# A cleared tile behind each gather, and less room for descriptors, in a graph-attention kernel

## The chip, the cores and the metric

The kernel runs on one core of one Trainium2 chip. Its engines are named as in the profile: PE (TensorE, with PEld for its weight loads), DVE (VectorE), ACT (ScalarE), POOL (GpSimd) and SP (SyncE). The metric is the device time of one launch in microseconds. The time before is 1312.44 us, the median of three runs.

## The reference

The kernel computes one layer of attention on a graph, a residual, and a second normalisation. There are N = 3125 nodes of 128 features, E = 100000 edges sorted by their destination, five relations and eight heads of 16 features. Cut to what matters:

```
for r in range(R):                        # five relations
    mask = edge_types == r
    q = x[dst] @ W_Q[r];  k = x[src] @ W_K[r];  v = x[src] @ W_V[r]   # per head
    logits = (q * k).sum(-1) / 4 + attn_bias[r]
    attn = softmax of logits over the edges of one destination with mask
    out += segment_sum(attn * v, dst)
h = out @ out_proj_w.T + out_proj_b + x
y = layernorm(h) * ln_gamma + ln_beta
return layernorm(x + y)
```

## The kernel before

**Rows instead of edges.** Keys and values are worked out once per node and relation and stored in device memory as `kv_d` (line 532 on), queries likewise as `q_d` (L714), the queries in three bf16 parts. For each tile of 128 edges, POOL fetches the 128 rows of keys and values with one indirect DMA (L865); the row numbers are in `idx`. The queries come as 120 consecutive rows (`qw`, L764, on SP's queue), which PE spreads over the edges with a matrix of zeros and ones (`hot`, L751; matmul L938).

**Steps.** The edges are cut into groups of 512 (four tiles). `NST` = 66 steps handle three groups each, the first only one. `tiles[k]` lists the tiles that step k gathers: 4, 12, 12 and then mostly 11, because in 63 steps one tile (the "early" tile) is not gathered but computed from rows of x that were fetched in the preparation: `early_turn` (L1052), `early_turned` (L1056), `early_rows` (PE, L1063) and `early_keep` (ACT, L1070). That makes 719 gathers in all. The rows of a step lie in one of four slots, two in `kv_early` and two in `kv_late` (made at L829, in memory that the preparation gave back).

**One step.** `products` (DVE, L951 and L958) multiplies keys with queries; `logits` (L999) sums over each head's features; PE turns the logits (L1031), DVE scans them for the maximum per destination (`scans`, L1076 and L1079), `less_max` (L1088), exponentials on ACT, turned back by PE (L1103); `weigh` (L1119) multiplies the values; `places` (ACT, L1132 and L1136) makes the matrix that `sums` (PE, L1146 and L1151) uses to add the edges of a node; `norm` (DVE, L1168 to L1172) divides; `relations` (PE, L1188) and `by_node` (ACT, L1192) put the result in order of nodes. Projection and the normalisations follow in blocks of 128 nodes.

**Order of the work.** The order is written out by hand in one loop over the steps; each engine runs its instructions in that order, and semaphores hold an instruction back until what it needs is there. The gathers are handed out at `POINTS` = 11 points a step. `point(k, j, leave)` issues as many gathers as are due with a lead of `KV_LEAD` = 2.0 steps, and `leave` is an instruction of the step behind which the gather is put. Points 6 to 10 of step k - 1 stand in step k before points 0 to 5 of k. For every step:

```
        point(k - 1, 6, products(k))
        point(k - 1, 7, weighted)
        ...
        point(k - 1, 8, logits(k))
```

**Startup.** The preparation (pools `load`, `work`, `pps` and others, closed together by `pre.close()`, L825) makes the tables. Its last instructions on DVE work out where the rows of each tile begin (L437 to L447) and count violations of the layout (L634 to L665); L671 to L673 add these up. The pool `flow` is opened behind `pre.close()`, so its tiles lie in memory that the preparation used. The gathers of steps 0 and 1 (16 of them) stand behind that in the text, but go to `kv_early`, which is memory of its own.

Of the kernel before, what the change touches and what calls it, by code (L numbers as in the profile page):

```python
# [9 lines left out]
F32 = mybir.dt.float32  # L10
# [8 lines left out]
P = 128  # L19
# [61 lines left out]
def gnn_kernel(  # L81
# [19 lines left out]
    with tc.manual_schedule():  # L101
        windowed_path(
            tc, n_bad_i, x, src, dst, edge_type, w_q, w_k, w_v, attn_bias, out_w, out_b,
            gamma, beta, out,
        )
# [37 lines left out]
def windowed_path(  # L143
# [4 lines left out]
    nc = tc.nc  # L148

    def behind(gather, other):  # L150
        if other is not None:
            tc.add_manual_dep(
                gather.ins,
                other.ins.name,
                mybir.DependencyInfo(mybir.DependencyClass.Sync, mybir.DependencyReason.DATA),
                reason="leave",
            )
# [673 lines left out]
    flow = ctx.enter_context(tc.tile_pool(name="flow", bufs=2))  # L831
# [5 lines left out]
    def runs(a, b):  # L837
        out_ = []
        for q in range(a, b):
            k = AT[q // T][0]  # L840
            kv, at = place(k)
            at += q - T * G0[k]
            if out_ and out_[-1][0] is kv and out_[-1][2] == at:
                out_[-1][2] += 1
            else:
                out_.append([kv, at, at + 1])
        return out_
# [9 lines left out]
        for k in range(NST)  # L857
    ]
    issued = []

    def gather(leave=None, n=1):
        for q in sum(tiles, [])[len(issued) :][: max(n, 0)]:
            ((kv, at, _),) = runs(q, q + 1)
            behind(
                nc.gpsimd.indirect_dma_start(  # L865
                    out=kv[:, at, :], out_offset=None, in_=kv_d[:, :],
                    in_offset=bass.IndirectOffsetOnAxis(
                        ap=idx[:, q % T, q // T : q // T + 1], axis=0
                    ),
                ),  # L870
                leave,
            )
            issued.append(q)

    def point(k, j, leave):
        at = k + (j + 1) / POINTS + KV_LEAD
        whole = min(int(at), NST)
        n = sum(len(t) for t in tiles[:whole])
        if whole < NST:
            n += int((at - whole) * len(tiles[whole]) + 1e-6)  # L880
        gather(leave, n - len(issued))
# [444 lines left out]
    q_at = {k: b for b, k in q_from.items()}  # L1326

    gather(n=len(tiles[0]))
    assert len(marks) >= len(tiles[1])
    for leave in marks[: len(tiles[1])]:  # L1330
# [675 lines left out]
```

## Time and profile before

| | |
|---|---|
| median of three runs | 1312.44 us (1310.02, 1320.14, 1312.44) |
| profiled execution, own time | 1318.95 us |
| its span, first to last instruction | 1317.2 us |
| mean granted TensorE clock | 0.838 |
| PE, DVE, ACT, POOL busy | 1006.5, 904.5, 689.3, 797.9 us |
| gathers L865 | 719, together 732.4 us on POOL |
| DMA packets of the gathers' queue | 36528, 98.42 MB |

The profile is one execution. A share of busy time is an average over the preparation, the 66 steps and the end. Rows give a line of the kernel, an engine, the operation, the tile written and the tile read, a count, the busy time and the mean of one; "<-" behind an idle time names what ended it, and "remote" or "another core or an unknown queue" says that nothing of this core that the profile sees did. "issue" is idle time for which the profile shows no wait. The busy time of a gather on POOL is the issuing of its descriptors; the rows land later.

### The profile page before, as it was taken

Reading aid. Unit: us, or ns where it says so; the run is one execution under the profiler, and the core shown is the slowest. Engines: PE = TensorE matmul, PEld = TensorE weight load, DVE = VectorE, ACT = ScalarE, POOL = GpSimd, SP = SyncE. Lnnn points to the kernel's source line nnn. Section 1 sums busy time; section 2 is a strip of 40 time slices with the busy share of each in tenths; the row PEclk is TensorE's granted clock in tenths of the full one; section 3 lists DMA queues with packets and bytes.
Section 4 is the critical chain, followed back from the end, with each engine's and each line's share of the span. In section 5 each row is a group of like instructions: output and inputs, shape, how many; then the busy total and the mean of one; then the engine's idle time right before and its main releaser. Section 6 shows DMA issues by size and latency. Waiting matters only on the chain.

```text
span 1317.2 us, 20087 instructions
## 1 busy us (share of the span) xinstructions
PE 1006.5 (76%) x5425; PEld 743.7 (56%) x5425; DVE 904.5 (69%) x1520; ACT 689.3 (52%) x1882; POOL 797.9 (61%) x793
## 2 busy tenths in 40 slices
PE   6984477988777877878788867777777877787776
PEld 3442355666565655656566655565555656566554
DVE  2545576768775777777776777686677677687776
ACT  1432255656565565546456646455555556465554
POOL 6664566666665666666665756665665566666650
PEclk9996679768888889888788888897888888878877
DMA  6884455555555555545555554555555455555440
GB/s 167 297 292 147 113 141 153 140 150 149 146 142 138 133 148 154 151 129 140 149 137 151 152 148 127 144 136 147 149 146 122 140 152 143 147 150 138 128 107 8
DMA packets 176110, 192.63 MB, mean 146 GB/s; under 512 B 121764, under 2 KB 137072, under 8 KB 175873
## 3 DMA queue, kind: packets, MB, share of 16 engines
q0 software_dynamic: 36528, 98.42, 28.4%
q1 hardware_dynamic: 138271, 91.97, 24.4%
q10 hardware_dynamic: 1194, 0.92, 0.3%
q8 instruction: 44, 0.72, 0.2%
q14 instruction: 73, 0.60, 0.2%
HBM read 160.80 MB, written 30.40 MB: 145 GB/s over the span
## 4 chain that ended last, share of the span: by engine, by line
PE 50%; DVE 16%; ACT 12%; another core or an unknown queue 11%; issue 9%; DMA 1%; SPq 1%; DVEq 0%; ACTq 0%
PE both L1151 14%; PE qe L1063 7%; PE lt L1052 5%; PE pr L522 5%; PE mid L1103 4%; ACT at L1132 4%; PE qe L938 3%; PE both L1146 3%; PE prq L896 2%; PE both L1188 2%; DVE wv L1119 2%; DVE mid L999 2%; DVE run L1076 2%; DVE run L1079 2%
## 5 line engine op out<-in xcount | busy, mean ns | idle before, releaser
L865 POOL DMA_INDIRECT kv_early<-kv_d,idx x366 | 372.2, 1017 | 217.6 <-issue 83.6
L865 POOL DMA_INDIRECT kv_late<-kv_d,idx x353 | 360.2, 1020 | 230.8 <-issue 70.0
L1151 PE MATMUL both<-wv,at 128*125 128x136 f32 x1544 | 326.3, 346 | 57.8 <-ACT oT L1192 24.8
L1151 PEld LDWEIGHTS both<-wv,at 128*125 128x125 f32 x1544 | 257.0, 230 | 142.9 <-issue 70.5
L1132 ACT ACTIVATE at<-wide_at,nkey 128x125 f32<-128x125 f32 x772 | 244.0, 391 | 0.0
L1063 PE MATMUL qe<-wkv,xr 128*128 128x256 f32 x630 | 162.4, 408 | 42.1 <-ACT xr L1056 24.7
L1076 DVE TENSOR_TENSOR_SCAN run<-mk,lt 120x640 f32<-120x640 bf16 (+1 forms) x66 | 97.8, 1482 | 105.6 <-remote 66.1
L1063 PEld LDWEIGHTS qe<-wkv,xr 128*128 128x128 f32 x630 | 124.0, 205 | 63.9 <-ACT xr L1056 27.9
L938 PE MATMUL qe<-qw,hot 120*128 120x128 bf16 x784 | 71.5, 257 | 76.8 <-ACT kv_late L1070 27.9
L1136 ACT ACTIVATE at<-at 128x500 f32<-128x500 f32 x193 | 119.6, 620 | 6.1
L938 PEld LDWEIGHTS <-hot 120*128 120x128 bf16 x784 | 66.7, 124 | 79.0 <-issue 78.4
L1188 PE MATMUL both<-rsum,o 125*128 125x25 f32 x380 | 59.7, 291 | 56.2 <-DVE o L1172 42.4
L1079 DVE TENSOR_TENSOR_SCAN run<-mk,run 120x640 f32<-120x640 bf16 (+1 forms) x66 | 98.5, 1492 | 2.3
L1052 PE MATMUL lt<-diag,xg 128*128 128x512 f32 x252 | 98.6, 520 | 0.0
L1103 PE MATMUL mid<-gather_heads,ls 120*128 120x24 f32 (+1 forms) x528 | 75.5, 283 | 22.6 <-ACT xTq L890 12.6
L999 DVE TENSOR_REDUCE mid<-kv_early 128x8 f32<-128x128 f32 (+3 forms) x51 | 61.3, 1202 | 45.6 <-ACT wv L1113 31.8
L1192 ACT COPY oT<-both 128x25 f32 x190 | 34.2, 180 | 111.4 <-PE both L1188 33.3
L1103 PEld LDWEIGHTS mid<-gather_heads,ls 120*128 120x128 f32 (+1 forms) x528 | 73.7, 215 | 29.6 <-ACT xTq L890 15.4
L1188 PEld LDWEIGHTS both<-rsum,o 125*128 125x128 f32 x380 | 53.6, 213 | 61.8 <-issue 56.5
L1146 PE MATMUL both<-wv,over 128*5 128x136 f32 x384 | 87.8, 316 | 0.0
L999 DVE TENSOR_REDUCE mid<-kv_late 128x8 f32<-128x128 f32 (+2 forms) x48 | 58.9, 1227 | 39.5 <-ACT wv L1113 29.1
L1168 DVE TENSOR_SCALAR both<-both 125x24 f32<-125x24 f32 (+1 forms) x65 | 12.1, 186 | 101.7 <-remote 49.2
(205 smaller groups left out, 1475.1 us busy)
## 6 DMA issues: line engine op xcount, KB each, us to landing
qw<-q_d SPq DMA_DIRECT2D x784, 30.0 KB
kt<-key_d SPq DMA_DIRECT2D x64, 360.0 KB
kv_d<-kvs SPq DMA_DIRECT2D x24, 640.0 KB
q_d<-q SPq DMA_DIRECT2D x25, 480.0 KB
mk<-msk_d SPq DMA_DIRECT2D x65, 150.2 KB
kv_early<-kv_d,idx POOLq DMA_INDIRECT x366
kv_late<-kv_d,idx POOLq DMA_INDIRECT x353
out<-z SPq DMA_DIRECT2D x24, 64.0 KB
```

The costliest lines, as they stand in the source:

```text
L865: nc.gpsimd.indirect_dma_start(out=kv[:, at, :], out_offset=None, in_=kv_d[:, :], in_offset=bass.IndirectOffsetOnAxis(ap=idx[:, q % T, q / ...
L938: spread = nc.tensor.matmul(dest[j], hot[:, j * P : (j + 1) * P], qw[:, j, :], start=True, stop=True)
L999: made = nc.vector.tensor_reduce(lg[:, n : n + c1 - c0], heads(kv[:, c0:c1, :H]), AX.X, ALU.add)
L1052: nc.tensor.matmul(lt[:, c0:c1], xg[:, e, :], at[:, c0:c1], start=True, stop=True)
L1063: nc.tensor.matmul(rows, xr[:, r * P : (r + 1) * P], wkv[:, r].rearrange("h s c -> h (s c)"), start=(r == 0), stop=(r == R - 1),)
L1076: there = nc.vector.tensor_tensor_scan(run[:n], mk[:n, :WIDE], lt, -BIG, op0=ALU.add, op1=ALU.max)
L1079: back = nc.vector.tensor_tensor_scan(run[:n, ::-1], mk[:n, WIDE:0:-1], run[:n, ::-1], -BIG, op0=ALU.add, op1=ALU.max)
L1103: nc.tensor.matmul(ex.rearrange("p (i t) k -> p t i k", t=T)[:, t], ls[: n * LANES, t * P : (t + 1) * P], gather_heads[: n * LANES, :n], s ...
L1132: nc.scalar.activation(at[:, t, :], row_at[:, :WR], AF.Abs, bias=nkey[:, t, g : g + 1], scale=1.0)
L1146: nc.tensor.matmul(pp[:R], over[:, g, :], live["wv", last][:, T * j + T - 1, :], start=False, stop=False,)
L1151: nc.tensor.matmul(pp[:WR], at[:, t, :], wv[:, T * i + t, :], start=(t == 0), stop=(t == end))
L1188: nc.tensor.matmul(nodes[:, i], o5[:, i], rsum[:WR], start=True, stop=True)
```

## The change

A tile `idle` of 128 columns and 128 partitions of float32 is taken from the pool `flow`. Behind each gather, POOL writes zeros into it; nothing reads it. In addition the room for descriptors of DMAs that are issued dynamically is set to 8192 bytes a partition.

```diff
     issued = []
+    idle = flow.tile([P, P], F32, name="idle", bufs=1)
 
     def gather(leave=None, n=1):
         for q in sum(tiles, [])[len(issued) :][: max(n, 0)]:
...
                 leave,
             )
             issued.append(q)
+            nc.gpsimd.memset(idle, 0.0)
...
-    nc = bacc.Bacc("TRN2", target_bir_lowering=False, num_devices=1)
+    nc = bacc.Bacc("TRN2", target_bir_lowering=False, num_devices=1, dynamic_dma_scratch_size=8192)
```

In the changed kernel a line behind the new ones has a number higher by one (from L860) or by two (from L874); the gather is L866 there and the memset L875.

## The prediction

> **What bounds the kernel now.** I read the page first: shares of busy time, the chain that ended last, the costliest groups.
>
> ```profile
> PE 1006.5 (76%) x5425; PEld 743.7 (56%) x5425; DVE 904.5 (69%) x1520; ACT 689.3 (52%) x1882; POOL 797.9 (61%) x793
> ...
> PE 50%; DVE 16%; ACT 12%; another core or an unknown queue 11%; issue 9%; DMA 1%; SPq 1%; DVEq 0%; ACTq 0%
> ...
> L865 POOL DMA_INDIRECT kv_early<-kv_d,idx x366 | 372.2, 1017 | 217.6 <-issue 83.6
> L865 POOL DMA_INDIRECT kv_late<-kv_d,idx x353 | 360.2, 1020 | 230.8 <-issue 70.0
> ```
>
> No engine is full, and POOL does not appear in the chain, though the 719 gathers (366 + 353) are nearly all it does. But 11% of the chain, some 145 of 1317.2 us, is put down to no engine at all. The waits show where it falls.
>
> ```profile
> DVE run L1076 <- remote: 66.1, 17, 10.7
> ...
> ACT kv_early L1070 <- remote: 57.2, 13, 7.7
> ...
> ACT kv_late L1070 <- remote: 53.0, 11, 6.7
> DVE both L1168 <- remote: 49.2, 15, 4.5
> ```
>
> The columns are total, times and longest. L1070 (`early_keep`), the scan L1076 and L1168 all wait for results of PE. L1070 waits in 13 + 11 = 24 steps, 110.2 us in all. One of them, in order of time (start, duration, what):
>
> ```profile
> 557.99 2.32 PE L1063 MATMUL qe<-wkv,xr 128*128 128x256 f32 x10
> ...
> 567.24 1.01 PE L938 MATMUL qe<-qw,hot 120*128 120x128 bf16 x8 [5.51 <-ACT kv_late L1070]
> ```
> ```profile
> 566.82 0.37 ACT L1070 COPY kv_late<-qe 128x256 f32<-128x256 f32 x1 [6.08 <-remote]
> ```
> ```profile
> 566.89 1.49 DVE L1076 TENSOR_TENSOR_SCAN run<-mk,lt 120x640 f32<-120x640 bf16 x1 [4.54 <-remote]
> ```
> ```profile
> 549.99 1.99 POOL L865 DMA_INDIRECT kv_early<-kv_d,idx  x1 [3.29 <-PE qe L938]
> 552.28 1.06 POOL L865 DMA_INDIRECT kv_early<-kv_d,idx  x1 [0.31 <-DVE ls L1088]
> ...
> 562.75 0.95 POOL L865 DMA_INDIRECT kv_early<-kv_d,idx  x1 [0.30 <-issue]
> 564.00 0.95 POOL L865 DMA_INDIRECT kv_late<-kv_d,idx  x1 [0.30 <-issue]
> 568.95 1.71 POOL L865 DMA_INDIRECT kv_late<-kv_d,idx  x1 [4.00 <-PE qe L938]
> ```
> ```profile
> 563.00:566.80 3.80, 0.00 (x0) 0.00 (x0) 0.00 (x0) 0.00 (x0) 1.64 (x2) 0.89 0.41 113
> ```
>
> The last row is a window: busy time of PE, PEld, DVE, ACT, POOL. For 3.8 us four engines do nothing and POOL issues its last two gathers. PE's matmuls had ended at 560.3 (557.99 + 2.32), yet ACT and DVE go on only at 566.8, which is 1.87 us after the last gather of the burst was issued (564.00 + 0.95 = 564.95). Then PE spreads the queries, and that releases the next gather at 568.95. The startup has the same picture:
>
> ```profile
> 101.97 0.94 POOL L865 DMA_INDIRECT kv_early<-kv_d,idx  x1 [5.14 <-DMA kt<-key_d]
> 103.22 0.95 POOL L865 DMA_INDIRECT kv_early<-kv_d,idx  x1 [0.30 <-issue]
> ...
> 118.22 0.95 POOL L865 DMA_INDIRECT kv_early<-kv_d,idx  x1 [0.30 <-issue]
> 122.51 0.94 POOL L865 DMA_INDIRECT kv_early<-kv_d,idx  x1 [3.34 <-DVE lrf L443]
> 123.76 0.95 POOL L865 DMA_INDIRECT kv_early<-kv_d,idx  x1 [0.30 <-DVE first L451]
> ```
> ```profile
> 113.12 1.48 PE L432 MATMUL rows<-ident,ends 99*1 99x99 f32 x8 [4.35 <-issue]
> ```
> ```profile
> 121.18 0.56 DVE L437 TENSOR_SCALAR first<-rows 1x396 int32<-1x396 f32 x1 [8.14 <-remote]
> ...
> 132.06 0.13 DVE L665 TENSOR_SCALAR vio<-last 1x1 f32<-1x1 f32 x1
> ...
> 134.64 0.28 DVE L951 TENSOR_TENSOR kv_early<-kv_early,qe 128x128 f32<-128x128 f32 x1
> ```
>
> L437 needs only L432's rows, there by 114.6 (113.12 + 1.48); it starts at 121.18, which is 2.01 us after the gather at 118.22 ended. So I read a **hold**: while gathers follow each other at 1.25 us, PE's signals arrive late, about 2 us after the last of them. The trace doesn't say why, and L1070 is named as held in 24 steps only. The bound, where there is a hold, is the length of POOL's burst: 549.99 to 564.95 for a step's 11 gathers.
>
> **The change, part by part.** *The memset.* It adds 719 instructions to POOL and none elsewhere; the others keep their counts and their order. Each waits only for the memset before it. The nearest row has the same shape and type:
>
> ```profile
> masks.py:197 POOL MEMSET ident<- 128x128 f32 x1 | 0.2, 204 | 0.4 <-POOLq L1993 0.4
> ```
>
> Back to back, gathers start 1.25 us apart (0.95 busy, 0.30 without a named wait). The memset adds at least 0 (it runs in those 0.30 us), at most 0.204 + 0.30 = 0.50 (each instruction has a gap of its own). I take 0.20, the duration of its row: period 1.45. A step then has 11 x 1.25 = 13.75 us of gathers before and 11 x 1.45 = 16.0 after. One step lasts
>
> ```profile
> L1076 DVE TENSOR_TENSOR_SCAN run<-mk,lt x66: 1477/1481/1489, 138.6 to 1291.0; 120x640 f32<-120x640 bf16 x65, 40x640 f32<-40x640 bf16 x1
> ```
>
> (1291.0 - 138.6) / 65 = 17.73 us, so POOL still fits, and where nothing is held the memsets lie beside PE's and DVE's work and cost nothing. Where a hold ends a step, the burst ends 11 x 0.204 = 2.2 us later, behind it ACT's L1070, PE's L938 and the next gather. Bounds: 0 (memset in the gap) and all 65 steps x 2.2 = 146. I take the 24 steps in which L1070 is held: **24 x 2.2 = 54 us**.
>
> *The startup.* `idle` comes from the pool `flow`, opened after `pre` is closed, so the first memset waits until the preparation no longer uses that memory; the last of these is L665 on DVE. Queued behind it on POOL are gathers 2 and on, which ran from 103.22 to 124.71. This delays them, and takes the hold of L437 away: the chain from L437 to L665 can begin at 114.7 instead of 121.18, so L665 comes at about 125.6 (132.06 - 6.5). Gathers 2 to 28 (steps 0 to 2 use 4, 12 and 12) then run from 126 at 1.45: number 17 is issued by 126 + 16 x 1.45 = 149, number 28 by 165; with 1.9 to land 151 and 167. (From 17 on they also hang behind products and scans of step 0, which need gathers up to 5; these land by 126 + 4 x 1.45 + 1.9 = 134, no later than now.) Who waits for them:
>
> ```profile
> 145.66 0.28 DVE L958 TENSOR_TENSOR kv_late<-kv_late,qe 128x128 f32<-128x128 f32 x1
> ...
> 159.80 1.49 DVE L1076 TENSOR_TENSOR_SCAN run<-mk,lt 120x640 f32<-120x640 bf16 x1 [10.72 <-remote]
> ...
> 164.30 1.75 DVE L958 TENSOR_TENSOR kv_late<-kv_late,qe 128x1536 f32<-128x1536 f32 x1
> ```
>
> The products of step 1 come 5 us later, those of step 2 about 3. If the burst also holds step 1's scan to its end, that is 126 + 28 x 1.45 + 2 = 168.6 against 159.80, 9 us. At 1.25 number 28 lands at 162, before it is wanted: -2. Bounds -2 and +9; I take **+6**, between the two products' delays and the held scan.
>
> *The port.* A gather stretches when two scans follow on DVE:
>
> ```profile
> 619.71 1.48 DVE L1076 TENSOR_TENSOR_SCAN run<-mk,lt 120x640 f32<-120x640 bf16 x1
> ...
> 623.41 0.87 DVE L751 TENSOR_SCALAR hot<-kt,row_in 120x512 bf16<-120x512 bf16 x3
> ```
> ```profile
> 621.31 2.16 POOL L865 DMA_INDIRECT kv_early<-kv_d,idx  x1 [0.30 <-issue]
> ```
>
> 2.16 instead of 0.95, so a memset may be held beside them or hold DVE: from 0 to one memset per step, 65 x 0.204 = 13 us. I take 0: in a step without a hold POOL has room for it. The Trainium skill ("SBUF — State Buffer", "Who interferes with whom") says that a DVE instruction with two SBUF inputs contends with GpSimd reads, not with an instruction that only writes, while a `tensor_scalar` in its 2-port mode locks GpSimd out and the reverse. The scan's row agrees that DVE can stretch POOL's work; no run here yet shows a memset beside it. By that rule only L751's three instructions could collide, and the sum would stay inside the same 13 us.
>
> *The room for descriptors.* A gather waits for the one eight before it (the semaphores rotate over eight), at 1.25 us each 10 us back; a gather lands, by the 1.87 and 2.01 us above, within an estimated 2. Few are under way, so I take 0. The bounds: below nothing isn't excluded, above it a ring that fills would show as POOL idle, at most the 0.50 per gather already taken as the upper price.
>
> *The sum.* The profiled execution's own time is 1318.95 us (span 1317.2): 1318.95 + 54 + 6 = 1379. It was 6.5 above the median of the runs shown (1312.44), so I say **1372**, 4.6% slower.
>
> **The rivals.**
> *Startup only.* The memset runs in the 0.30 us gap, or the lead of two steps absorbs it. For it: 16.0 of 17.73 us fits, and POOL isn't in the chain. Against: the 24 holds that end with a burst. Time: 1312.4 + 6 = 1318.
> *The memset breaks the hold.* If signals of PE are late because POOL issues gathers without a break, a pause of another kind between them may let them through. For it: both holds shown lie in bursts and end with them. Against: a gap of 0.30 us is there already and lets nothing through. Price: L1070's 110.2 us at most, half of it 55, and the startup's 6 gone or turned to a gain: 1312.4 - 55 = 1257; all of it 1202.
> *POOL becomes the bound.* At 0.50 a gather the period is 1.75, 11 of them 19.3 us against 17.73: 65 x 1.6 = 102, with 9 of startup 1423. It decides from 17.73 / 11 = 1.61 a gather on, that is a memset above 0.36. If every step is held, 0.20 is enough: 1312.4 + 146 + 6 = 1464.
>
> **How the numbers follow.** Longer bursts 0.41; startup only 0.15; hold broken 0.30; POOL the bound 0.14. A measurement of this kernel tells about 1% (13 us) from no change. Faster: the broken hold, 0.30 less a little that stays under 13 us, 0.28. Same: 0.15 and those bits, 0.17. Slower: 0.55. The likeliest case alone spans 1335 (11 steps held) to 1415 (44). The range for 8 in 10 reaches into the broken hold as far as its half price and into the bound POOL: 1255 to 1440.
>
> **What would show it.** In the profile after: memsets of about 0.20 us and gathers starting 1.45 apart in a burst (1.25: startup only; 1.61 or more: POOL the bound); gather 2 at about 126, L437 at about 115 and L665 near 126; the first products of step 1 near 151; the waits of L1070 on "remote" up from 110.2 to about 160, as many or more. If they fall well below 110 the hold is broken and I am wrong on the sign. If L437 is still late with no gather beside it, my reading of the hold is wrong altogether.

## The result and the profile after

The changed kernel takes 1324.37 us (median of 13 runs, 1319.69 to 1335.45), the kernel before 1312.06 us in as many runs on the same chip. The ratio is 1.0102, with a 95% interval of 1.0075 to 1.0128: slower by 1.0%, some 12 us. Forecast were 1372 us and 4.6%. The profiled execution of the changed kernel took 1320.82 us, its span is 1319.0 us.

The page after, in the same parts as before (shares of busy time, the chain, the costliest groups). The shares of this chain add up to 72%, because it could be followed back from the end only to 360 us; they can't be set beside those of before, which cover the whole span.

```profile
PE 1029.5 (78%) x5425; PEld 757.2 (57%) x5425; DVE 910.1 (69%) x1520; ACT 691.7 (52%) x1882; POOL 957.4 (73%) x1512
...
PE 38%; DVE 10%; ACT 7%; another core or an unknown queue 7%; issue 6%; SPq 2%; DMA 1%; POOL 1%; ACTq 0%; DVEq 0%; POOLq 0%
...
L866 POOL DMA_INDIRECT kv_early<-kv_d,idx x366 | 376.3, 1028 | 131.3 <-issue 57.9
L866 POOL DMA_INDIRECT kv_late<-kv_d,idx x353 | 359.0, 1017 | 135.0 <-issue 50.6
L875 POOL MEMSET idle<- 128x128 f32 x719 | 158.5, 220 | 22.6 <-DVE vio L665 22.2
```

POOL gained 159.5 us of busy time (957.4 - 797.9) and the kernel 12. The gathers' idle time fell from 448 us (217.6 + 230.8) to 266, so most of the clearings lie where POOL was idle before. The start, in POOL's order of time:

```profile
100.93 0.94 POOL L866 DMA_INDIRECT kv_early<-kv_d,idx  x1 [4.85 <-DMA kt<-key_d]
124.10 0.21 POOL L875 MEMSET idle<- 128x128 f32 x1 [22.23 <-DVE vio L665]
124.77 0.95 POOL L866 DMA_INDIRECT kv_early<-kv_d,idx  x1 [0.46 <-issue]
...
132.94 0.95 POOL L866 DMA_INDIRECT kv_early<-kv_d,idx  x1 [0.17 <-issue]
133.88 0.22 POOL L875 MEMSET idle<- 128x128 f32 x1
134.27 0.95 POOL L866 DMA_INDIRECT kv_early<-kv_d,idx  x1 [0.17 <-issue]
```

The first clearing waits 22.23 us for L665, and gather 2 starts at 124.77 instead of 103.22. Then gathers start 134.27 - 132.94 = 1.33 to 1.34 us apart. The gap ahead of a gather fell from 0.30 to 0.17 us, so of a clearing of 0.22 us only 0.09 is added. On DVE:

```profile
112.16 0.56 DVE L437 TENSOR_SCALAR first<-rows 1x396 int32<-1x396 f32 x1 [1.59 <-PE rows L432]
...
123.68 0.13 DVE L665 TENSOR_SCALAR vio<-last 1x1 f32<-1x1 f32 x1
...
150.83 0.28 DVE L960 TENSOR_TENSOR kv_late<-kv_late,qe 128x128 f32<-128x128 f32 x1
...
165.12 1.49 DVE L1078 TENSOR_TENSOR_SCAN run<-mk,lt 120x640 f32<-120x640 bf16 x1 [10.86 <-PE mid L887]
```

L437 comes 9 us earlier, L665 8.4. The products of step 1 are 5.2 us later than before (145.66) and its scan 5.3 (159.80). The line of all scans, and the waits of L1072 and L1194 (L1070 and L1192 before; the first of these rows is from the profile before):

```profile
L1078 DVE TENSOR_TENSOR_SCAN run<-mk,lt x66: 1477/1486/1489, 139.2 to 1293.2; 120x640 f32<-120x640 bf16 x65, 40x640 f32<-40x640 bf16 x1
```
```profile
ACT oT L1192 <- remote: 13.4, 4, 4.1
```
```profile
ACT oT L1194 <- remote: 70.7, 15, 6.8
...
ACT kv_early L1072 <- remote: 49.0, 11, 6.4
...
ACT kv_late L1072 <- remote: 43.2, 7, 8.1
```

A step lasts (1293.2 - 139.2) / 65 = 17.75 us, against 17.73 before. L1072 waits 92.2 us in 18 steps, where 110.2 in 24 were measured before and about 160 forecast. L1194 waits 57 us more than L1192 did; over all engines the waits that end by "remote" fell from 350 to 304 us. The 54 us of the steps did not come. The spans of the two profiles lie only 1.8 us apart (1317.2 and 1319.0), so this pair doesn't show the 12 us of the medians either.

### The profile page after: what moved, and what is told of

It reads as the page before. It is cut to its first block, busy times and chain, and to the rows that moved or that the text cites. A ratio compares the mean times of both kernels' runs of the same rounds, so it can differ in the third digit from the quotient of the medians.

```text
span 1319.0 us, 20802 instructions
## 1 busy us (share of the span) xinstructions
PE 1029.5 (78%) x5425; PEld 757.2 (57%) x5425; DVE 910.1 (69%) x1520; ACT 691.7 (52%) x1882; POOL 957.4 (73%) x1512
## 4 chain that ended last, share of the span: by engine, by line
PE 38%; DVE 10%; ACT 7%; another core or an unknown queue 7%; issue 6%; SPq 2%; DMA 1%; POOL 1%; ACTq 0%; DVEq 0%; POOLq 0%
PE both L1153 13%; PE qe L1065 5%; PE lt L1054 5%; PE mid L1105 4%; PE both L1148 3%; ACT at L1134 2%; PE qe L940 2%; DVE wv L1121 2%; DVE run L1081 2%; DVE run L1078 2%; PE lt L1033 2%; PE prq L898 2%; PE both L1190 2%; ACT at L1138 1%
## 5 line engine op out<-in xcount | busy, mean ns | idle before, releaser
L866 POOL DMA_INDIRECT kv_early<-kv_d,idx x366 | 376.3, 1028 | 131.3 <-issue 57.9
L866 POOL DMA_INDIRECT kv_late<-kv_d,idx x353 | 359.0, 1017 | 135.0 <-issue 50.6
L1153 PE MATMUL both<-wv,at 128*125 128x136 f32 x1544 | 348.8, 364 | 96.3 <-ACT oT L1194 69.7
L1153 PEld LDWEIGHTS both<-wv,at 128*125 128x125 f32 x1544 | 273.7, 244 | 187.2 <-ACT oT L1194 84.7
L875 POOL MEMSET idle<- 128x128 f32 x719 | 158.5, 220 | 22.6 <-DVE vio L665 22.2
L1065 PE MATMUL qe<-wkv,xr 128*128 128x256 f32 x630 | 153.9, 393 | 12.6 <-ACT xr L1058 5.7
L1054 PE MATMUL lt<-diag,xg 128*128 128x512 f32 x252 | 108.9, 566 | 0.0
L1194 ACT COPY oT<-both 128x25 f32 x190 | 34.2, 180 | 141.2 <-remote 70.7
L1105 PE MATMUL mid<-gather_heads,ls 120*128 120x24 f32 (+1 forms) x528 | 84.2, 302 | 22.2 <-ACT xTq L892 11.0
L1105 PEld LDWEIGHTS mid<-gather_heads,ls 120*128 120x128 f32 (+1 forms) x528 | 83.2, 239 | 29.8 <-ACT xTq L892 14.7
L1081 DVE TENSOR_TENSOR_SCAN run<-mk,run 120x640 f32<-120x640 bf16 (+1 forms) x66 | 98.4, 1491 | 2.3
L367 POOL DMA_INDIRECT xg<-in_x,xi x60 | 60.0, 999 | 28.9 <-issue 17.5
L1054 PEld LDWEIGHTS lt<-diag,xg 128*128 128x128 f32 x252 | 54.8, 241 | 42.4 <-issue 42.3
L522 PE MATMUL pr<-wkv,xT 128*128 128x512 f32 x150 | 65.3, 574 | 15.6 <-issue 7.8
```

The source lines that it names most:

```text
L866: nc.gpsimd.indirect_dma_start(out=kv[:, at, :], out_offset=None, in_=kv_d[:, :], in_offset=bass.IndirectOffsetOnAxis(ap=idx[:, q % T, q / ...
L875: nc.gpsimd.memset(idle, 0.0)
L1054: nc.tensor.matmul(lt[:, c0:c1], xg[:, e, :], at[:, c0:c1], start=True, stop=True)
L1065: nc.tensor.matmul(rows, xr[:, r * P : (r + 1) * P], wkv[:, r].rearrange("h s c -> h (s c)"), start=(r == 0), stop=(r == R - 1),)
L1081: back = nc.vector.tensor_tensor_scan(run[:n, ::-1], mk[:n, WIDE:0:-1], run[:n, ::-1], -BIG, op0=ALU.add, op1=ALU.max)
L1105: nc.tensor.matmul(ex.rearrange("p (i t) k -> p t i k", t=T)[:, t], ls[: n * LANES, t * P : (t + 1) * P], gather_heads[: n * LANES, :n], s ...
```

## The experiments

The experiments ran in five sets, each on another chip; the kernel before takes 1084 to 1086 us on each of them, some 230 us less than on the first, and no trace of theirs has a row that names "remote". Each ratio below is to the kernel before on the same chip in the same set. The record doesn't name the chip of the first measurement; "the first chip" below stands for that measurement, be it the chip or the moment that differs. The difference of 230 us turned out to be the most useful fact of the study: the same change costs another amount where the kernel before is faster.

**The two parts of the change, apart.** The room alone:

```diff
-    nc = bacc.Bacc("TRN2", target_bir_lowering=False, num_devices=1)
+    nc = bacc.Bacc("TRN2", target_bir_lowering=False, num_devices=1, dynamic_dma_scratch_size=8192)
```

> Only the smaller room for descriptors, no tile and no clearing. If the 12 us of the change come from the startup (gathers 2 on wait for the end of the preparation) or from the 0.09 us that each clearing adds to a gather's period (1.34 against 1.25 in a burst), this kernel is the kernel before: 1312, within 5 us, gathers 1.25 apart. If the room or the moved tiles matter, it takes some of the 12 us: 1318 to 1324, and POOL idles longer between gathers.

Measured: 1082.1 us, ratio 0.9972 (0.9940 to 1.0004). The room costs nothing that shows. The clearings alone, with the old room, were not tried. The trace of this kernel, which issues the same instructions as the kernel before, is also the reference for that chip:

```profile
DVE 42%; DMA 18%; PE 15%; issue 13%; POOL 6%; ACT 4%; SPq 1%; DVEq 0%; ACTq 0%; POOLq 0%
```
```profile
L1076 DVE TENSOR_TENSOR_SCAN run<-mk,lt x66: 1477/1480/1487, 110.1 to 1054.5; 120x640 f32<-120x640 bf16 x65, 40x640 f32<-40x640 bf16 x1
```
```profile
L865 POOL DMA_INDIRECT kv_late<-kv_d,idx x353 | 364.9, 1034 | 114.0 <-issue 71.6
L865 POOL DMA_INDIRECT kv_early<-kv_d,idx x366 | 362.8, 991 | 113.7 <-issue 74.0
```
```profile
90.65 0.95 POOL L865 DMA_INDIRECT kv_early<-kv_d,idx  x1 [0.30 <-DVE ends L426]
91.90 0.94 POOL L865 DMA_INDIRECT kv_early<-kv_d,idx  x1 [0.30 <-issue]
93.15 0.95 POOL L865 DMA_INDIRECT kv_early<-kv_d,idx  x1 [0.30 <-DVE frf L442]
```
```profile
92.18 0.56 DVE L437 TENSOR_SCALAR first<-rows 1x396 int32<-1x396 f32 x1 [1.59 <-PE rows L432]
```

A step lasts 14.53 us there. The chain names POOL and DMA, which the first one hardly did: the gathers' landing is on it. POOL sat idle before the 719 gathers for 114.0 + 113.7 = 227.7 us, 0.32 us each, hardly more than the gap of 0.30: here POOL issues gathers almost without a pause, where the first profile left 448 us. And L437 follows PE after 1.59 us with gathers back to back on both sides of it. On this chip a burst of gathers does not hold PE's results.

**The wait and the clearings, apart.** Two kernels, one edit of the change in each; the words behind # name the kernel.

```diff
-            nc.gpsimd.memset(idle, 0.0)
+            if len(issued) == 1:                        # first_only
+                nc.gpsimd.memset(idle, 0.0)
...
-    idle = flow.tile([P, P], F32, name="idle", bufs=1)
+    idle = keep("idle", [P, P])                         # own_tile: in the pool const, from the start
```

> The change with one clearing behind the first gather only; the other 718 are left out. Startup theory: gather 2 still starts at about 124.8, the scan of step 2 is still some 5 us late (181.4 against 176.8), and the time is most of the change's: 1317 to 1324. Per-gather theory (0.09 us a gather in steps that end with a burst, 24 x 11 x 0.09 = 24 us at most): near the kernel before, 1310 to 1315, and the 12 us come back with the clearings alone. In both L437 starts at about 112, if the gathers beside it were what held it.

> The change with the cleared tile in memory of its own, so that the first clearing waits for nothing; 719 clearings as in the change. Startup theory: gather 2 starts at about 102 as before, the time goes back to 1312 to 1317. Per-gather theory: it stays at 1320 to 1326. L437 should be held again to about 2 us after the last gather of its burst, that is to about 122 or 123.

Measured: first_only 1093.6 us, 1.0104 (1.0050 to 1.0158); own_tile 1140.74 us, 1.0520 (1.0469 to 1.0571). So the wait costs about 10 us and the clearings about 55. Both expectations for L437 were too simple: it was unheld on this chip whatever stood beside it. In first_only the wait has the form that it has in the change:

```profile
103.69 0.20 POOL L876 MEMSET idle<- 128x128 f32 x1 [17.81 <-DVE vio L665]
104.36 0.95 POOL L866 DMA_INDIRECT kv_early<-kv_d,idx  x1 [0.46 <-issue]
```

Its steps are as long as the reference's, (1063.2 - 118.2) / 65 = 14.54 us, and it starts them 8.1 us later. own_tile starts them at 112.4, and a step takes (1119.0 - 112.4) / 65 = 15.49 us:

```profile
L1079 DVE TENSOR_TENSOR_SCAN run<-mk,lt x66: 1477/1480/1489, 118.2 to 1063.2; 120x640 f32<-120x640 bf16 x65, 40x640 f32<-40x640 bf16 x1
```
```profile
L1078 DVE TENSOR_TENSOR_SCAN run<-mk,lt x66: 1477/1479/1489, 112.4 to 1119.0; 120x640 f32<-120x640 bf16 x65, 40x640 f32<-40x640 bf16 x1
```

That is 0.96 us a step, close to 11 gathers x 0.09. With no slack on POOL, its period sets the step on this chip.

**The change itself on such chips, and repeats.** The kernels of the next set are the changed kernel (after_2), the two above once more, and a clearing behind every second gather (`if len(issued) % 2:`).

> The changed kernel itself, beside the kernel before on the chip of this set. Where no hold appears (kernel before about 1085, steps of 14.4 us): POOL is the bound, each clearing adds 0.09 us to a gather's period, 65 x 11 x 0.09 = 64 us, and the startup some of its 10: 5 to 7% slower. Where the holds appear (kernel before about 1312, steps of 17.7 us): 11 gathers of 1.34 are 14.7 us and fit, so only the startup's 5 us and a few more: 0.5 to 1.5% slower.

> The clearings without the wait of the first one. POOL-bound theory: where steps are 14.4 us, 4.5 to 6% slower again; where they are 17.7, within 0.5% of the kernel before or faster than the change by 5 us. Held-burst theory as first predicted: 1 to 4% slower where holds appear.

> Only the wait of the first clearing, without the other 718. Startup theory: 10 us slower where no hold appears (as in the first set), some 5 us slower where holds appear, because the gathers that come later also leave L437 unheld.

> The change with a clearing behind every second gather, 360 in all; the others are left out. If POOL's period sets the step, its price is half: 65 x 5.5 x 0.09 = 32 us and the startup's 10 where steps are 14.4 us, 3 to 4.5% slower. Where steps are 17.7 us, like first_only: 0 to 1%.

Measured: after_2 1154.88 us, 1.0667 (1.0627 to 1.0708); own_tile_2 1.0558 (1.0510 to 1.0606); first_only_2 1.0113 (1.0075 to 1.0150); every_second 1121.24 us, 1.0378 (1.0329 to 1.0427). The change is 6.7% slower here, and 11 us of wait and 59 of clearings add up to its 71. Half the clearings leave 26 us beside the wait, nearly half the price. The chain of after_2 has POOL in it:

```profile
DVE 26%; PE 20%; POOL 20%; DMA 15%; issue 9%; ACT 7%; SPq 3%; POOLq 0%; DVEq 0%; ACTq 0%
```
```profile
L1078 DVE TENSOR_TENSOR_SCAN run<-mk,lt x66: 1478/1481/1489, 118.4 to 1122.1; 120x640 f32<-120x640 bf16 x65, 40x640 f32<-40x640 bf16 x1
```

A step lasts (1122.1 - 118.4) / 65 = 15.44 us: what POOL needs for its gathers, clearings and the stretches under scans. That is less than the 17.73 of the first profile, and more than the 14.53 here.

**What a clearing costs.** Two behind each gather; one of one column (`idle[:, 0:1]`); one of 512 columns (`[P, 4 * P]`).

> The change with two clearings behind each gather, 1438 in all. Period of a gather in a burst 1.34 + 0.22 = 1.56 or somewhat more, 11 of them 17.2 us against a step of 17.7. If longer bursts hold back PE's results, as predicted: 24 steps x 11 x 0.22 = 58 us more than the change, about 1380. If the lead of two steps takes up what POOL loses as long as 11 gathers fit in a step: 1324 to 1332. If POOL is the bound already: 65 x 11 x 0.22 = 157 more, 1480.

> The change with one column cleared instead of 128. If a clearing costs by its columns: it takes about 0.11 instead of 0.22 us, the period is 1.25 or below, and only the startup's 10 us are left, 1 to 1.5% slower than the kernel before. If it costs by being one more instruction: period 1.34 and 6 to 7% slower, like the change.

> The change with 512 columns cleared instead of 128. By its columns: a clearing of about 0.5 us, period about 1.62, 65 x 11 x 0.28 = 200 us more than the change. If, as with the two clearings (period 1.93, where 1.56 was expected), the gap of 0.17 us ahead of a gather also grows to 0.50: period 1.95, like two clearings, 43% slower than the kernel before.

Measured: two_clears 1548.75 us, 1.4288 (1.4221 to 1.4355); thin_clear 1101.2 us, 1.0163 (1.0121 to 1.0205); wide_clear 1357.04 us, 1.2527 (1.2474 to 1.2580). POOL in order of time, thin_clear, wide_clear and two_clears:

```profile
407.69 0.94 POOL L866 DMA_INDIRECT kv_early<-kv_d,idx  x1 [0.19 <-issue]
408.62 0.12 POOL L875 MEMSET idle<- 128x1 f32 x1
408.94 0.94 POOL L866 DMA_INDIRECT kv_early<-kv_d,idx  x1 [0.19 <-issue]
```
```profile
406.68 0.95 POOL L866 DMA_INDIRECT kv_early<-kv_d,idx  x1 [0.17 <-issue]
407.63 0.55 POOL L875 MEMSET idle<- 128x512 f32 x1
408.34 0.96 POOL L866 DMA_INDIRECT kv_early<-kv_d,idx  x1 [0.16 <-issue]
```
```profile
399.81 0.95 POOL L866 DMA_INDIRECT kv_late<-kv_d,idx  x1 [0.50 <-issue]
400.76 0.22 POOL L875 MEMSET idle<- 128x128 f32 x1
401.04 0.20 POOL L876 MEMSET idle<- 128x128 f32 x1
401.74 0.95 POOL L866 DMA_INDIRECT kv_late<-kv_d,idx  x1 [0.50 <-issue]
```

The columns decide. A clearing of 0.12 us leaves the period at 1.25. One of 0.55 makes it 1.66, and 65 x 11 x (1.66 - 1.34) = 229 us more than the change compares with 202 measured (1357.04 - 1154.88, two chips). So of one clearing some 0.12 to 0.14 us is free, and the rest counts in full. Two clearings are not one of double length: the period is 1.93 us where 1.56 was expected, because the gap ahead of the gather is 0.50 instead of 0.17. Of the three outcomes expected of two_clears, the highest was 157 us more than the change; 394 were measured (1548.75 - 1154.88, two chips).

**A longer step.** If POOL's slack decides, the price must fall where steps are long. DVE's instructions L1119 and L999 issued twice with the same result (`for _ in range(2):` around each), in the kernel before and in the changed one:

> The kernel before with two of DVE's instructions of each step issued twice (the weighing L1119 and the sum over features L999, about 1.75 us each, with the same result), so that a step of 14.4 us becomes about 17.5 to 18, as long as the steps of the profile that the prediction was made from. About 1085 + 65 x 3.4 = 1305, between 1270 and 1320.

> The change, with the same two instructions issued twice. POOL-slack theory: 11 gathers and clearings take 11 x 1.34 = 14.7 us and some 1.5 us that scans stretch them, 16.2 in all, which fits in a step of 17.5 to 18; only the startup's 5 to 10 us are left, slower than slowed_before by 0 to 1.2%, as the change measured 1.0%. If clearings cost by themselves, whatever the length of a step (a port, or a burst that holds others): 4 to 6% slower than slowed_before.

Measured: 1247.15 us, 1.1526 (1.1470 to 1.1582), and 1270.74 us, 1.1727 (1.1678 to 1.1776). The second is 1.9% above the first, more than the upper end expected and far from 6.7%. The steps are 17.09 and 17.22 us. Of the 16 us between the profiled executions (spans 1253.2 and 1269.4), 9 lie in the steps and 7.5 in the start. The medians are 24 us apart; the other 7 lie between executions, as the profiled one of slowed_before took 1254.96 us, 8 above its median. Why a step became 0.13 us longer although POOL's 15.44 us fit was not found. Then a set that asked whether the first measurement can be had again, with a clearing of one column in a tile of its own (own_thin):

> The changed kernel once more. Where the kernel before takes about 1312: 1.0% slower, as measured first. Where it takes about 1085: 6.7% slower, as measured last (POOL sets the step).

> The clearings without the wait of the first. Where the kernel before takes about 1312, startup theory: equal to it within 0.5%; clearing theory: 0.5 to 1% slower, like the change. Where it takes about 1085: 5.4% slower.

> Only the wait of the first clearing. Where the kernel before takes about 1312, startup theory: 0.4 to 1% slower; clearing theory: equal within 0.3%. Where it takes about 1085: 1.1% slower.

> One column cleared behind each gather, in a tile of its own. The clearing of 0.12 us fits into the gap of 0.30 us (period 1.25, as in thin_clear), and nothing waits at the start: equal to the kernel before within 0.6%, on either chip. If the 719 instructions cost anything by themselves, as thin_clear's 1.6% against first_only's 1.1% may hint: 0.5% slower.

The chip was again one with a fast kernel before (1084.72 us). Measured: after_3 1.0636 (1.0591 to 1.0681), own_tile_3 1.0523 (1.0480 to 1.0565), first_only_3 1.0114 (1.0076 to 1.0151), own_thin 1090.65 us, 1.0032 (1.0004 to 1.0060). 719 further instructions that fit in the gap cost a third of a per cent, at most 0.6. Last, steps that are long because PE has more to do; unlike on the first chip, no result of PE is held here:

```diff
-        turn_logits(k)
+        for _ in range(6):
+            turn_logits(k)
```

> The kernel before with PE's turning of the logits (L1031, 0.8 us) issued six times instead of once in each step, with the same result, so that scan, L1070 and L1168 get PE's results 4 us later and ACT and DVE idle meanwhile. About 1085 + 65 x 3.3 = 1300, between 1250 and 1345; step 17 to 18.5 us.

> The change with the same repeated turning. POOL-slack theory: 11 x 1.34 + 1.5 = 16.2 us of POOL's work fit in the step, so a step is as long as in late_pe_before (within 0.1 us) and only the start's 5 to 10 us are left: 0.3 to 1.2% slower than late_pe_before, like the 1.0% first measured. If late results of PE and longer bursts add up, as predicted: 24 to 65 steps x 1 us, 2 to 5.5% slower.

Measured: 1199.31 us, 1.1045 (1.0998 to 1.1091), and 1207.59 us, 1.1129 (1.1082 to 1.1177): 8.3 us or 0.7% between the two. The repeats lengthened a step less than expected, to 16.2 us, and that was enough:

```profile
L1076 DVE TENSOR_TENSOR_SCAN run<-mk,lt x66: 1479/1487/1489, 117.7 to 1172.1; 120x640 f32<-120x640 bf16 x65, 40x640 f32<-40x640 bf16 x1
```
```profile
L1078 DVE TENSOR_TENSOR_SCAN run<-mk,lt x66: 1479/1486/1489, 124.4 to 1179.1; 120x640 f32<-120x640 bf16 x65, 40x640 f32<-40x640 bf16 x1
```
```profile
PE 76%; ACT 13%; DVE 6%; DMA 2%; issue 2%; POOL 1%; DVEq 0%; POOLq 0%; ACTq 0%
```

16.22 us a step without and 16.23 with 719 clearings: they cost nothing there. The first scan comes 6.7 us later, and that is what is left. POOL needs 15.44 a step, PE sets 16.2, and POOL has 1% of the chain (the last row, of late_pe_after).

## Why the prediction was wrong

**The step that failed** is "24 x 2.2 = 54 us", the longer burst behind a hold. It says two things: that PE's results come late beside gathers, and that a longer burst makes them later and the step longer.

The first was read rightly from the first chip's trace, and in more than the two places shown. All 24 held L1070 start 0.80 to 2.04 us after a gather has ended, none while one is issued. Which of the two causes the other stays open: in these places the next gather mostly waits for something that is held too or follows from the held result.

The second did not hold. Bursts became longer by 11 x 0.09 = 1 us a step, and the steps stayed at 17.73 and 17.75 us. Nor does a hold last as long as the burst. In the changed kernel 8 of the 18 held L1072 start while a further gather is issued, this one with another gather of the burst behind it:

```profile
518.60 0.95 POOL L866 DMA_INDIRECT kv_late<-kv_d,idx  x1 [0.17 <-issue]
...
519.93 0.95 POOL L866 DMA_INDIRECT kv_late<-kv_d,idx  x1 [0.17 <-issue]
```
```profile
519.27 0.37 ACT L1072 COPY kv_late<-qe 128x256 f32<-128x256 f32 x1 [3.60 <-remote]
```

On other chips gathers hold nothing: the same gathers stood beside L437 in room_only and it wasn't late. The late_pe pair, with longer bursts and steps 0.01 us apart, has no held results, so it shows the slack and not the hold.

**The price of a clearing** was mis-sized: 0.20 of its duration taken as cost, of bounds 0 to 0.50; measured 0.09, since 0.13 of its 0.22 lies in the gap. With 0.09 the same step would have given 24 x 11 x 0.09 = 24 us, which was still not there in the steps.

**The startup** was right in its order: the wait for L665, gather 2 near 126 (124.77), L665 near 126 (123.68), the products of step 1 near 151 (150.83). The last is right partly by luck: gather 17 was issued by 147 instead of 149, and DVE waited until 149.29 for rows of `kv_early`, the last of which are those of gather 16. That is 3.7 us after its issue had ended, where 1.9 us were allowed for the landing. The scan of step 1 came 5.3 us later, for which +6 was taken, but this isn't yet a time at the end: scan by scan, the profile after stands 4.6 to 12.9 us behind the one before from step 1 to step 49, and 2.2 at the last scan. Where the wait was run alone, on the other chips, it cost 1.0 to 1.1%, that is 11 to 12 us. That L437 would be early (115, measured 112.16) was right. The reason given, that no gathers stand beside it, fits the first chip and was not tested there.

**The rivals.** "Startup only" gave 1318 us, and the steps of the pair of profiles agree with it; the measured 12 us are above its 6. It had been given 0.15, against the longer bursts' 0.41, although the row that speaks for it, 16.0 of 17.73 us, stood in the text. The room at 0 was right, as far as room_only shows. "POOL becomes the bound" was worked out to decide from 17.73 / 11 = 1.61 us a gather; that holds for a step of 17.73 us. On a chip with steps of 14.53 the same reckoning gives 1.32, and the change's 1.34 is past it, but by 65 x 11 x 0.02 = 14 us only, where 55 to 59 were measured. What it leaves out is that gathers stretch under scans: the 719 gathers of room_only are busy for 727.7 us, 48 more than at their median of 0.946 us each, 0.7 us a step. With them 13.75 becomes 14.5, the whole step. "The memset breaks the hold" may have come true in part, as 8 of 18 holds ended inside a burst where none of 24 did; that the clearings did it isn't shown, and the steps did not become shorter. And the forecast's lower end for the longer bursts, 1335 for 11 steps held, is too low by its own sum: 1312 + 6 + 11 x 2.2 = 1342.

**The port** cost nothing that shows on the first chip: clearings take 207 to 274 ns in the changed kernel, medians of 218, and L751 341 where it took 348.

```profile
L875 POOL MEMSET idle<- x719: 207/218/274, 124.1 to 1277.2; 128x128 f32 x180
```

The Trainium skill ("SBUF — State Buffer", "Who interferes with whom") says that an instruction of GpSimd which only writes isn't held by a DVE instruction with two SBUF inputs. The trace agrees: no clearing of the changed kernel is held for the 1.49 us of a scan, and the 26 that start beside the second scan (L1081) take at most 0.23 us, while gathers beside it still take up to 2.08. On another chip one case fits the collision with L751 that the prediction mentions: in after_2 one clearing of the 719 took 0.94 us, from 122.11 on, while DVE ran L751 three times from 122.05 on.

**What stays open.** "remote" on the first chip stands for late results of PE. The profile records when PE raises the counter that others wait on. In the profile before, 294 of 1113 such records come more than 1.5 us after the last PE instruction that raises it has ended, in the one after 320 of 1147; in every other trace it is 1 or 2 of over 1200. DVE's and ACT's counters are never so late in more than 3 records. Whether the signal was late or PE's end is recorded too early isn't to be seen, and why the first chip has it was not found; no trace of the later runs shows it. The granted clock doesn't explain it: 0.838 in the profile before, and 0.831 in slowed_before, which has no such wait. So the 12 us of the first measurement were not taken apart on that chip. That they are the start's 5 to 7 us and a remainder spread over executions is argued from its trace and from late_pe (0.7%), not shown: the wait alone was not run there.

## What to carry to other kernels

An instruction added to an engine with slack costs the difference between what the engine then needs per step and what the step takes, and little below it (0.01 us a step at 16.2, 0.13 at 17.1); so find the step's length and the engine's need first (here 15.44 against 14.53, 16.22 or 17.73 us) before pricing any single wait. A wait that a profile puts down to nothing it knows is no ground for a causal price, however regular its end looks; look for one place where the supposed cause is there and the effect isn't, and for one where the effect ends while the cause goes on. And a new tile from a pool that reuses memory brings a wait with it: giving it memory of its own takes off 12 us of 71 here, and one column instead of 128 takes off most of the rest.

## What the runs showed of the hardware that was not expected

The 0.30 us between two gathers on POOL can hold another instruction: a clearing of 0.12 us there leaves the period at 1.25 us. A second clearing does not only add its 0.20: the gap ahead of the next gather grows from 0.17 to 0.50 us, and the period from 1.34 to 1.93.

The same program takes 1312 us in one measurement and 1084 to 1086 in five later ones, each of these on another chip, with steps of 17.73 us in the first and 14.53 in room_only; the share of the chain that no engine explains (11%) is gone in all the later traces. In the first a quarter of PE's signals are recorded over 1.5 us late (294 of 1113), but hardly any of DVE's (3 of 774) or ACT's (1 of 728). A change measured at 1.0% there costs 6.4 and 6.7% in two of the others.

A gather beside a scan with two inputs in SBUF took up to 2.08 us instead of 0.95; the 26 clearings that started beside one took at most 0.23.
